# Issuing the sampling weights' four loads of a half band one a slot, right behind the preceding product of weights

## The chip, the core and the metric

The kernel runs on one core of one Trainium2 chip. The metric is the device time of one launch in microseconds; before the change it is 9640.8 us (median of three runs, 9635.6 to 9673.78). All arithmetic is fp32. The engines are named as in the profile: PE (matrix products), PEld (its weight loads), DVE (elementwise work on vectors), ACT (activations and copies), POOL (elementwise work and its own transfers) and SP, which only issues transfers (DMAs).

## The reference

Two layers work on 32 images of 96 channels, 56x56. Layer 0 is an inverted-residual block: a 1x1 convolution to 576 channels, batch norm and SiLU, a depthwise 3x3 convolution, batch norm and SiLU, a squeeze-and-excite gate, a 1x1 convolution back to 96 channels, and the residual. Layer 1 computes magnitudes of a 2-D real FFT of its input, from them and from channel sums a channel gate and a spatial gate, the gated image y, then a 3x3 convolution of y and four coordinate planes that yields 18 offsets and a gate, a plain 3x3 convolution of y, and a deformable one:

```python
y = x * ca * sa
offset = _conv(aux, off_w, off_b, (1, 1))
y_base = _conv(y, base_w, base_b, (1, 1))
px = xx + off[:, :, 0]; py = yy + off[:, :, 1]
sampled = _grid_sample_taps(y, px, py)          # bilinear, 9 taps a pixel
y_def = jnp.einsum('bcthw,oct->bohw', sampled, def_w.reshape(c, c, 9))
z = (1 - gate) * y_base + gate * y_def
```

z is then normalised over the whole batch, x is added, and a ReLU follows.

## The kernel before

**What is computed for the weights.** An image is worked in 7 bands of 8 rows (`bands`, 224 in all), and each band in two halves of 28 columns (h = 0, 1; 448 halves). The bilinear sampling is done by PE: for a 4x4 tile of pixels and one tap each, the values come from an 8x8 block of y around the tile, and the sample is a product of that block (`yt`, 64 positions by 96 channels, transposed from a copy `ybl` of y) with a table of weights over the 64 positions. The weight of a position is a row factor times a column factor. `offsets` makes the factors: PE convolves (`joint_conv`, L605 and L633), DVE copies the offsets out of PSUM (`at`, L651), POOL writes them to DRAM (`od`, L655), SP reads them back spread over partitions (`ht`, L667), ACT turns them into hat functions in two passes (L670, L671), and ACT writes these to DRAM (`hd`, L674). `weights_load` then reads each half's factors back, widened over the 64 positions: `wc` (column factors) and `wr` (row factors), each in two transfers, four of 252 KB for a half, all issued by SP (L685, L686). `weights` multiplies them on DVE (L692, 128x1008, in place in `wc`), and `sample_tiles` uses the product as the moving operand of 14 matrix products (L721; the profile has two rows for each fp32 product), 6 of them in the half's first part, 8 behind its third slot.

**Order.** The main loop runs over the 224 bands and the two halves. A half has 7 slots, a band 17 (7, 7, and 3 behind the halves). In each slot one step of `offsets` for the band after next is issued (`next(more)`), and `pump` issues what is due of two other streams that work on other images: `second(b + 1)` (the rest of layer 0 and the FFTs: transfers `hq` L305, `x2` L361) and `first(b + 2)` (layer 0's depthwise convolution, with DVE's long row L261, transfers `xt` L212 and, from ACT, `h2d` L223). `refill` (transfers `yp` L584 and L596) comes behind the last slot of a band. SP's queue is in exactly this written order (`manual_schedule`), and a transfer that has to wait holds up all that stand behind it. On the other engines a scheduler orders the instructions from their dependences and its own estimate of when their inputs are there; so the place of a product on DVE follows from where its loads are written.

**Buffers.** `wc` has three (READY + AHEAD + 1), `wr` two (AHEAD + 1). Call L the running number of a half, and (j, h) its band in the image and its half. The loads of half L can be issued when `hd` of its band has landed, the tile products of half L-3 have been read out of the `wc` buffer (L721), and the product of half L-2 has been read out of the `wr` buffer (L692). At the top of half L-1 `prepare` issues all four loads of half L; behind the third slot of half L-1 its product is issued. The steps of `offsets` for band n + 2 run during band n: its `od` is issued in the first slots, its `ht` in the first slot of the second half, and its `hd` behind the fourteenth slot.

The transfers of SP and of ACT share eight completion semaphores in turn; an issue waits for the one that used its semaphore eight transfers before.

Of the kernel before, what the change touches and what calls it, by code (L numbers as in the profile page):

```python
# [64 lines left out]
AHEAD = 1  # L65
READY = 1
# [50 lines left out]
def bank(p):  # L117
    return p["mm"].tile([128, 512], FP, name="mm")
# [559 lines left out]
def weights_load(nc, p, hd, h):  # L678

    src = hd.rearrange("n i t k -> n i (t k)")[:, :, h * NTH * KP : (h + 1) * NTH * KP]  # L680
    wc = p["wc"].tile([2 * NS, NTH * KP], FP, name="wc")
    wr = p["wr"].tile([2 * NS, NTH * KP], FP, name="wr")
    for s in range(2):
        ps = slice(s * NS, (s + 1) * NS)
        nc.sync.dma_start(wc[ps], src[2 * s].unsqueeze(0).to_broadcast([SB, SB, NTH * KP]))  # L685
        nc.sync.dma_start(wr[ps], src[2 * s + 1].unsqueeze(1).to_broadcast([SB, SB, NTH * KP]))  # L686
    return wc, wr


def weights(nc, wc, wr):  # L690

    nc.vector.tensor_tensor(wc, wc, wr, ALU.mult)  # L692
    return wc


def block_channels(nc, p, yp, j, h):

    yt = p["yt"].tile([2 * NS, NTH, C], FP, name="yt")
    yb = p["ybl"].tile([C, NTH, 2, SB, SB], FP, name="ybl")
    src = yp[:C, j * RB : j * RB + SB, h * NTH * TS : h * NTH * TS + SB]  # L700
    for s in range(2):
        blocks = bass.AP(src.tensor, src.offset + s * TS * WY, [src.ap[0], [TS, NTH], [WY, SB], [1, SB]])
        nc.gpsimd.tensor_copy(yb[:, :, s], blocks)  # L703
    for lo, hi in ((0, 4), (4, NTH)):
        pt = bank(p)
        for t in range(lo, hi):
            nc.tensor.transpose(pt[:, (t - lo) * C : (t - lo + 1) * C], yb[:, t].rearrange("c s r x -> c (s r x)"),  # L707
                                p["w"]["ident"][:C, :C])
        nc.scalar.copy(yt[:, lo:hi].rearrange("p t c -> p (t c)"), pt[:, : (hi - lo) * C])  # L709
    return yt  # L710


def sample_tiles(nc, p, yt, s, v, group):


    pts = [(bank(p), bank(p)) for _ in group]
    for (lo, hi), pt in zip(group, pts):
        for t in range(lo, hi):
            for k in range(2):
                ps = slice(k * NS, (k + 1) * NS)  # L720
                nc.tensor.matmul(pt[k][:C, (t - lo) * KP : (t - lo + 1) * KP], yt[ps, t], s[ps, t * KP : (t + 1) * KP],  # L721
                                 start=True, stop=True)
    for (lo, hi), pt in zip(group, pts):
        for k in range(2):
            nc.scalar.copy(v[:C, :, lo:hi, k].rearrange("c k t p -> c t k p"),  # L725
                           pt[k][:C, : (hi - lo) * KP].rearrange("c (t k p) -> c t k p", t=hi - lo, k=NTAP))


def pack(nc, v):

    for i in range(3):
        nc.scalar.copy(v[C:, 1 + 2 * i : 3 + 2 * i], v[i * QC : (i + 1) * QC, KA:])  # L732
# [25 lines left out]
def gates_of(nc, p, hid):  # L758

    pgs = bank(p), bank(p)  # L760
    for i, pg in enumerate(pgs):
        ps = slice(i * NS, i * NS + DMID)
        nc.tensor.matmul(pg[:C, :BW], p["w"]["dg2p"][ps], hid[ps], start=True, stop=True)
    return [gate_from(nc, p, pg) for pg in pgs]
# [174 lines left out]
def layers(tc, a, dp, x1d, zd, stats, far):  # L939
# [6 lines left out]
    nc = tc.nc  # L946
    B = x1d.shape[0]
    with ExitStack() as ctx:
        p = {"tc": tc, "dp": ctx.enter_context(tc.tile_pool(name="l1d", bufs=3, space=DRAM))}
# [28 lines left out]
        def flush():  # L978
            while later:
                later.pop(0)[1]()  # L980
# [27 lines left out]
        def start(b, length):  # L1008
            streams[:] = [[second(b + 1), 0, n_second, slot + 3, slot + length - 8],
                          [first(b + 2), 0, n_first, slot, slot + length]]  # L1010

        def pump():
            nonlocal slot
            slot += 1
            for st in streams:
                due = st[2] * min(1.0, (slot - st[3]) / (st[4] - st[3]))
                while st[1] < due:
                    st[1] += 1
                    next(st[0], None)
            later.sort(key=lambda e: e[0])  # L1020
            while later and later[0][0] <= slot:
                later.pop(0)[1]()

        def drain():
            for st in streams:
                for _ in st[0]:
                    pass
# [3 lines left out]
        def refill(b, upto):  # L1031

            upto = min(H, upto)
            r = filled.get(("y", b), 0)
            while ("sa", b) in p and r < upto:
                r1 = min(upto, r + RB)
                args = load_rows(nc, p, yp, b, x1d[b], r, r1)
                later.append((slot + 4, lambda args=args: attend_rows(nc, p, b, *args)))
                r = filled["y", b] = r1
            r = filled.get(("fq", b), 0)  # L1040
            if ("fq", b) in p and r < upto:
                load_freq(nc, p, yp, b, r, upto)
                filled["fq", b] = upto
# [11 lines left out]
        def end_half(n, h, v, gate, st):  # L1055
            if h == 0:
                pds[n] = p["pd"].tile([128, 512], FP, name="pd")
            deform(nc, p, pds[n], v, h)
            if h:
                pd = pds.pop(n)  # L1060
                later.append((slot + 2, lambda: join(n, pd, gate, st)))
# [12 lines left out]
        hids, gates, ybs, hds, ready = [], [], [], [], []  # L1074

        def find(n):
            if n % 2 == 0:
                hids.append(p["hid"].tile([2 * NS, BW], FP, name="hid"))
            hid = hids[n // 2][n % 2 * NS : n % 2 * NS + DMID]
            return offsets(nc, p, yp, bands[n][1], top[:, n % NBD : n % NBD + 1], hid, ybs, hds)  # L1080
# [6 lines left out]
        flush()  # L1087
        p.pop("diag")
        n_loads = 0
        loads = []  # L1090

        def prepare(upto):

            nonlocal n_loads
            while n_loads < min(upto, 2 * len(hds)):
                n, m = divmod(n_loads, 2)
                loads.append(weights_load(nc, p, hds[n], m))
                n_loads += 1

        prepare(READY + AHEAD)  # L1100
        for _ in range(READY):
            ready.append(weights(nc, *loads.pop(0)))
        yts = [block_channels(nc, p, yp, 0, 0)]
        start(0, turn * (NTX + 2))
        for n, (b, j) in enumerate(bands):
            if j == 0:
                st = p["st"].tile([C, NBD, 6], FP, name="st")
            if j == turn:
                drain()
                refill(b + 1, j * RB - PD)  # L1110
                flush()
                start(b + 1, slots)
            more = find(n + 2) if n + 2 < len(bands) else iter(())
            next(more, None)
            for h in range(2):
                v = p["vp"].tile([128, NTAP, NTH, 2, TP], FP, name="v")
                prepare(2 * n + h + READY + AHEAD)
                s = ready.pop(0)
                yt = yts.pop(0)
                for i, group in enumerate(GROUPS):  # L1120
                    sample_tiles(nc, p, yt, s, v, group)
                    for _ in range(group[0][0], group[-1][1]):
                        next(more, None)
                        pump()
                    if i == 0:
                        for end in ends:
                            end()
                        ends.clear()
                        if h == 1 and n + 1 < len(bands):
                            yts.append(block_channels(nc, p, yp, bands[n + 1][1], 0))  # L1130
                        ready.extend(weights(nc, *ws) for ws in loads[:1])
                        del loads[:1]
                        if h == 0:
                            yts.append(block_channels(nc, p, yp, j, 1))
                pack(nc, v)
                if h == 0:
                    if n % 2 == 0:
                        gates.extend(gates_of(nc, p, hids[n // 2]))
                    gate = gates.pop(0)
                ends.append(lambda n=n, h=h, v=v, gate=gate, st=st: end_half(n, h, v, gate, st))  # L1140
            for _ in more:
                pass
            pump()
            pump()
            pump()
            if b + 1 < B:
                refill(b + 1, (j + 1) * RB - PD if j < NBD - 1 else H)
            if j == NBD - 1:
                nc.vector.tensor_reduce(top[:, NBD:], top, AX.X, ALU.max)
# [350 lines left out]
```

## Time and profile before

| | |
|---|---|
| median of three runs | 9640.8 us (9635.6 to 9673.78) |
| profiled execution | 9648.5 us, span 9646.7 us, mean granted PE clock 0.923 |
| PE busy | 8472.7 us (88%) |
| DVE busy | 7227.2 us (75%) |
| ACT busy | 5322.1 us (55%) |
| POOL busy | 2532.6 us (26%) |
| moved by DMA | 1485.98 MB, 154 GB/s over the span |
| products of weights (L692, DVE) | 448 times, 564.6 us busy, 704.2 us idle just before them |

The time of the profiled execution is that of the span and 1.8 us around it. Shares of busy time are over the whole span; the main loop is the stretch from about 480 us to 9350 us, 282 us an image, with a start of one image's layer 0 ahead of it and the normalisation behind it. PE's spans count its own time for a matrix product; the granted clock says in what part of full speed these ran. A row of the waits gives the engine and line that waited, who ended the wait, the sum in us, how often, and the longest.

### The profile page before, as it was taken

How to read it: one execution, taken by the hardware profiler on the slowest of the kernel's cores; microseconds unless marked ns; L12 is line 12 of the kernel's file. 1: busy time of each engine (PE TensorE's matmuls, PEld its weight loads, DVE VectorE, ACT ScalarE, POOL GpSimd, SP SyncE). 2: the span in 40 equal slices, each digit the busy share in tenths (PEclk: the TensorE clock that was granted, in tenths of full speed). 3: DMA queues.
4: the chain of work that ended last, by engine and by line, in shares of the span. 5: the costliest groups of instructions: out<-in, count | busy, mean ns of one | idle time of the engine just before them, and what ended most of it. 6: DMA issues, size and time to landing. Idle time of an engine off the chain costs nothing. (4 is left out here: it accounts for less than half of the span.)

```text
span 9646.7 us, 129705 instructions
## 1 busy us (share of the span) xinstructions
PE 8472.7 (88%) x48374; PEld 5064.2 (52%) x48374; DVE 7227.2 (75%) x6948; ACT 5322.1 (55%) x10262; POOL 2532.6 (26%) x2642
## 2 busy tenths in 40 slices
PE   6889989998999999999899989999999999999870
PEld 3455555555555555555555555555555555555540
DVE  7688777778777787877777887777878777777323
ACT  2355555565555556555555655555555555565453
POOL 1123223222222322222232322233222323322210
PEclk9899999999999999999999999999999999999985
DMA  2355555555555555555555555555555555554449
GB/s 94 95 143 148 151 152 160 150 149 143 147 155 154 160 154 145 145 149 155 154 160 155 145 142 153 151 158 154 153 139 145 150 157 157 153 152 135 130 154 417
DMA packets 1069473, 1485.98 MB, mean 154 GB/s; under 512 B 590438, under 2 KB 840086, under 8 KB 1056550
## 3 DMA queue, kind: packets, MB, share of 16 engines
q1 hardware_dynamic: 858747, 985.20, 37.9%
q10 hardware_dynamic: 153803, 329.80, 9.2%
q0 software_dynamic: 56288, 162.60, 6.7%
q8 instruction: 388, 6.36, 0.3%
q14 instruction: 247, 2.02, 0.1%
HBM read 1064.29 MB, written 412.65 MB: 153 GB/s over the span
## 5 line engine op out<-in xcount | busy, mean ns | idle before, releaser
L261 DVE SCALAR_TENSOR_TENSOR acch<-hp,w,acch 128x1512 f32<-128x1512 f32 (+1 forms) x2250 | 4320.5, 1920 | 32.8
L605 PE MATMUL mm<-yp,c_jointW 104*128 104x448 f32 x4032 | 1649.0, 561 | 9.0 <-ACT yt L709 5.5
L740 PE MATMUL pd<-v,c_def 128*96 128x224 f32 (+1 forms) x6272 | 1414.8, 376 | 127.6 <-ACT v L732 104.1
L703 POOL COPY ybl<-yp 96x448 f32<-96x448 f32 x896 | 1014.7, 1159 | 1903.7 <-PE mm L707 1903.3
L721 PE MATMUL mm<-wc,yt 64*96 64x144 f32 x12544 | 1168.1, 308 | 153.5 <-DVE yb L638 76.8
L740 PEld LDWEIGHTS pd<-v,c_def 128*96 128x96 f32 (+1 forms) x6272 | 1051.8, 173 | 437.4 <-ACT v L732 142.5
L168 PE MATMUL mm<-xt,w 96*128 96x392 f32 (+3 forms) x2688 | 1136.3, 561 | 133.8 <-ACT yt L709 96.0
L605 PEld LDWEIGHTS mm<-yp,c_jointW 104*128 104x128 f32 x4032 | 783.6, 196 | 806.0 <-issue 762.6
L721 PEld LDWEIGHTS mm<-wc,yt 64*96 64x96 f32 x12544 | 884.2, 167 | 489.8 <-issue 188.0
L221 ACT ACTIVATE acch<-acch,sh,inv 128x1568 f32<-128x1568 f32 x288 | 487.5, 1693 | 1159.0 <-DVE acch L261 1143.9
L692 DVE TENSOR_TENSOR wc<-wc,wr 128x1008 f32<-128x1008 f32 x448 | 564.6, 1260 | 704.2 <-DMA wr<-hd 690.5
L725 ACT COPY v<-mm 96x288 f32<-96x288 f32 (+1 forms) x2688 | 1003.6, 442 | 117.7 <-PE mm L721 78.9
L172 ACT ACTIVATE hp<-mm,sh,inv 128x392 f32<-128x392 f32 (+2 forms) x1216 | 811.8, 672 | 326.9 <-PE mm L168 282.1
L633 PE MATMUL mm<-yp,c_base0W 96*64 96x448 f32 x4032 | 913.5, 550 | 0.0
L323 PE MATMUL mm<-hq,w3s 128*96 128x392 f32 x2048 | 788.2, 531 | 127.4 <-DMA hq<-h2d 125.9
L655 POOL DMA_DIRECT2D od<-at x224 | 186.3, 832 | 2275.1 <-DVE at L651 1451.9
L732 ACT COPY v<-v 32x448 f32<-32x448 f32 x1344 | 755.3, 562 | 30.3
L168 PEld LDWEIGHTS mm<-xt,w 96*128 96x128 f32 (+1 forms) x2688 | 389.9, 189 | 495.1 <-issue 264.8
L709 ACT COPY yt<-mm 128x384 f32<-128x384 f32 (+1 forms) x896 | 350.9, 441 | 491.5 <-PE mm L707 489.4
L323 PEld LDWEIGHTS mm<-hq,w3s 128*96 128x96 f32 x2048 | 336.3, 173 | 477.7 <-issue 382.5
L466 POOL TENSOR_TENSOR o<-o,xc 96x392 f32<-96x392 f32 x256 | 396.5, 1549 | 643.9 <-ACT o L333 642.3
L633 PEld LDWEIGHTS mm<-yp,c_base0W 96*64 96x64 f32 x4032 | 294.6, 134 | 515.5 <-issue 490.2
(194 smaller groups left out, 9023.7 us busy)
## 6 DMA issues: line engine op xcount, KB each, us to landing
h2d<-acch ACTq DMA_DIRECT2D x288, 784.0 KB
wc<-hd SPq DMA_DIRECT2D x896, 252.0 KB
wr<-hd SPq DMA_DIRECT2D x896, 252.0 KB
hq<-h2d SPq DMA_DIRECT2D x128, 980.0 KB
hq<-h2d SPq DMA_DIRECT2D x128, 784.0 KB
x<-x1d SPq DMA_DIRECT2D x768, 98.0 KB
ht<-od SPq DMA_DIRECT2D x224, 252.0 KB
hd<-ht ACTq DMA_DIRECT2D x224, 252.0 KB
```

The lines of the kernel that those rows point to most:

```text
L168: nc.tensor.matmul(pt[p0 : p0 + w1.shape[1], : rows * W], w1, xts[hf][:, r0 * W : (r0 + rows) * W], start=True, stop=True)
L172: nc.scalar.activation(h1[lo:hi, row0 : row0 + rows, 1 : 1 + W], pt[lo:hi, : rows * W].rearrange("p (h w) -> p h w", h=rows), AF.Silu, bia ...
L261: nc.vector.scalar_tensor_tensor(acc[:, lo:hi], win, wk, acc[:, lo:hi], ALU.mult, ALU.add)
L323: nc.tensor.matmul(pts[half][:C, :EW], w3s[:, ch], hq, start=(i == 0), stop=False)
L605: nc.tensor.matmul(view, weights[:, k], yp[:channels, r0 : r0 + RB, dx + PD - 1 : dx + PD - 1 + W], start=(k == 0), stop=(k == NTAP - 1))
L633: nc.tensor.matmul(pb[k % 2 * BC : (k % 2 + 1) * BC, :BW].rearrange("p (h w) -> p h w", h=RB), w["base"][:, k], yp[:C, r0 : r0 + RB, dx + ...
L692: nc.vector.tensor_tensor(wc, wc, wr, ALU.mult)
L703: nc.gpsimd.tensor_copy(yb[:, :, s], blocks)
L721: nc.tensor.matmul(pt[k][:C, (t - lo) * KP : (t - lo + 1) * KP], yt[ps, t], s[ps, t * KP : (t + 1) * KP], start=True, stop=True)
L725: nc.scalar.copy(v[:C, :, lo:hi, k].rearrange("c k t p -> c t k p"), pt[k][:C, : (hi - lo) * KP].rearrange("c (t k p) -> c t k p", t=hi - ...
L732: nc.scalar.copy(v[C:, 1 + 2 * i : 3 + 2 * i], v[i * QC : (i + 1) * QC, KA:])
L740: nc.tensor.matmul(out.rearrange("c q (t x) -> c t q x", x=TS), p["w"]["def"][ks, k], v[ks, k].rearrange("c t s (r x) -> c t (s r) x", r=T ...
```

## The change

`weights_load` becomes a generator: it takes the two tiles first, and then issues one transfer a step. `prepare` puts the generator into a list `spread`; `spread_load` advances it. `prepare` is called behind the product of half K+1 (third slot of half K), for half K+2, where it was called at the top of half K for half K+1. In each later slot one transfer is issued ahead of that slot's other work, so the four transfers of a half stand in slots 3, 4, 5 and 6 of the half two before it. A call ahead of the product issues what should be left. The first two halves' loads are issued at once, as before. Number and size of the transfers, the buffers and the products stay as they are.

```diff
@@ weights_load
+    yield wc, wr
     for s in range(2):
         ps = slice(s * NS, (s + 1) * NS)
         nc.sync.dma_start(wc[ps], src[2 * s].unsqueeze(0).to_broadcast([SB, SB, NTH * KP]))
+        yield
         nc.sync.dma_start(wr[ps], src[2 * s + 1].unsqueeze(1).to_broadcast([SB, SB, NTH * KP]))
-    return wc, wr
+        yield
@@ layers
-        loads = []
+        loads, spread = [], []
+
+        def spread_load(steps):
+            for _ in range(steps):
+                while spread and next(spread[0], spread) is spread:
+                    spread.pop(0)
 
         def prepare(upto):
 
             nonlocal n_loads
             while n_loads < min(upto, 2 * len(hds)):
                 n, m = divmod(n_loads, 2)
-                loads.append(weights_load(nc, p, hds[n], m))
+                spread.append(weights_load(nc, p, hds[n], m))
+                loads.append(next(spread[-1]))
                 n_loads += 1
 
         prepare(READY + AHEAD)
+        spread_load(8 * (READY + AHEAD))
@@ the main loop
                 v = p["vp"].tile([128, NTAP, NTH, 2, TP], FP, name="v")
-                prepare(2 * n + h + READY + AHEAD)
                 s = ready.pop(0)
                 yt = yts.pop(0)
                 for i, group in enumerate(GROUPS):
                     sample_tiles(nc, p, yt, s, v, group)
                     for _ in range(group[0][0], group[-1][1]):
+                        spread_load(1)
                         next(more, None)
                         pump()
@@ behind the third slot of a half
+                        spread_load(4)
                         ready.extend(weights(nc, *ws) for ws in loads[:1])
                         del loads[:1]
+                        prepare(2 * n + h + 1 + READY + AHEAD)
```

## The prediction

> **What bounds the kernel now.** I read the page's busy times, then the waits of the engines and of SP's queue, and then one image in the timeline. "Place (j, h)" below is the product for half h of band j of an image.
>
> ```profile
> PE 8472.7 (88%) x48374; PEld 5064.2 (52%) x48374; DVE 7227.2 (75%) x6948; ACT 5322.1 (55%) x10262; POOL 2532.6 (26%) x2642
> ...
> L692 DVE TENSOR_TENSOR wc<-wc,wr 128x1008 f32<-128x1008 f32 x448 | 564.6, 1260 | 704.2 <-DMA wr<-hd 690.5
> ```
>
> ```profile
> DVE wc L692 <- DMA wr<-hd: 690.5, 152, 18.3
> ...
> PE mm L323 <- DMA hq<-h2d: 125.9, 31, 9.4
> ...
> PE mm L707 <- ACT sq L413: 80.3, 21, 6.5
> ```
>
> PE is the limit: between 480 and 9350 us it is busy 8124 of 8870 us. The product's 690 us are DVE's; they count only where they starve PE. They are not spread evenly. Summed by place over the images, 182 us lie at (2,1), 182 at (6,0), 102 at (1,0), 97 at (0,0), and 132 at the ten others. PE's idle time in the loop, 739 us, lies elsewhere: I followed each gap over 0.3 us back through its releasers, and 171 us at (2,1) end at a late `wr`, 125 us at (0,0) at a late `hq`, 47 us at (1,0) at a late `ht`; 312 us end at no transfer. At (6,0), where DVE waits longest, PE idles 0.0 us. One image (the seventeenth), at (2,1), in the timelines of SP, DVE, ACT and PE:
>
> ```profile
> 5060.03 0.57 SPq L686 DMA_DIRECT2D wr<-hd  x1
> 5074.72 0.66 SPq L667 DMA_DIRECT2D ht<-od  x1
> 5075.48 0.57 SPq L685 DMA_DIRECT2D wc<-hd  x1
> ...
> 5077.59 0.57 SPq L686 DMA_DIRECT2D wr<-hd  x1
> ```
>
> ```profile
> 5079.67 1.04 DVE L259 TENSOR_SCALAR acch<-hp,w 128x1568 f32<-128x1568 f32 x1
> 5089.44 1.21 DVE L692 TENSOR_TENSOR wc<-wc,wr 128x1008 f32<-128x1008 f32 x1 [8.73 <-DMA wr<-hd]
> ```
>
> ```profile
> 5091.29 1.00 ACT L413 ACTIVATE sq<-mm 128x464 f32<-128x464 f32 x2 [9.64 <-DVE s L414]
> ```
>
> ```profile
> 5091.90 0.74 PE L707 MATMUL mm<-c_ident,ybl 96*128 96x96 f32 x3 [6.19 <-ACT sq L413]
> ```
>
> SP stands at `ht` until `od` has landed (issued 5067.61, landed 5074.70, behind eight weight loads issued from 5055.6 to 5060.6); the loads of (2,1) follow it and land at 5089.31. DVE, which executes in order, stops at the product 8.73 us; ACT waits for DVE, PE for ACT. Of DVE's stop 2.5 us are hidden from PE. And PE is slow afterwards (columns: busy us of PE, PEld, DVE, ACT, POOL; granted clock; DMA share; GB/s):
>
> ```profile
> 5060.00:5083.00 23.00, 23.00 (x205) 13.62 (x204) 19.96 (x21) 14.31 (x28) 4.83 (x4) 1.00 0.53 136
> ...
> 5089.00:5106.00 17.00, 11.68 (x33) 6.34 (x34) 15.34 (x12) 13.02 (x24) 2.67 (x2) 0.51 0.09 26
> ```
>
> The granted clock is 1.00 before the gap and 0.51 for 17 us behind it. In the records of the loop it is either 1.0 or 0.5, and an L605 product follows the last after 0.383 us at 1.0, after 0.750 us at 0.5. So half of PE's busy time at half clock is lost: 271 us busy so at (2,1) cost 135 us, 114 at (0,0) 57 us, 48 at (1,0) 24 us.
>
> **The change, part by part.** It issues the same 1792 loads (0.57 to 0.60 us each on SP, which has time) and runs the same 448 products. What moves is their place.
>
> On SP, in the order in which the changed program stands: the loads of (1,0) come ahead of six `x2` loads and those of (1,1) ahead of six or four more; (0,0)'s first load ahead of an `hq`; (0,1)'s ahead of an `hq` (the first of them) and three refills; (3,1)'s ahead of six `x2` and three refills; (4,0)'s ahead of two or four `x2`; (6,0)'s and (6,1)'s among the two `hq`; (3,0)'s and (5,0)'s ahead of `xt`. Those of (2,0) and (2,1) pass nothing. On DVE the products move forward: by 14.7 us at (1,0), 12.4 at (2,0), 10.3 at (5,1), 10.1 at (6,0), 5 to 6 at (0,1), (1,1), (4,0), 2 to 5 at (0,0), (4,1), (6,1) (medians: time between the end of the row that will precede it and its present arrival), and not at (2,1), (3,0), (3,1), (5,0). A product that moves forward gains only if its loads move as far.
>
> *Place (2,1).* Its neighbours stay. But ahead of it (1,1)'s loads come some 7 to 19 us sooner, so the burst of eight is gone: `od`, whose usual landing takes 3.2 us (the page's median), no longer takes 7.1, and `ht` is free 3.9 us sooner, less 1.2 us since (1,1)'s product now stands ahead of `at`. The buffer of `wc` is the next limit: the tile products of (1,0) end at 5072.87, so the loads go at 5072.9 and not 5075.5. 2.6 us sooner at least, 4.3 if the transfers ahead are done too; 3.5 x 31 images = 108 us of PE's idle 171 (bounds 0 and 171). The clock's part in the same proportion: 85 of 135 us.
>
> *Place (0,0).* The `hq` that PE waits 3.81 us for landed 13.2 us after its issue, behind another `hq` (980 KB), four weight loads and an `ht`. Two of the four, 504 KB, now go ahead of the waiting first `hq`. At the 3024 KB that went from 4988.8 to 5007.25 (164 KB/us) that is 3.1 us; I take 2.7 x 31 = 85 us (bounds 62, at the window's 256 GB/s, and 125), and 35 us of clock.
>
> *Place (1,0).* ACT waits for an `ht` that was issued behind four loads and took 10.5 us; a lone one took 3.8 us (issued 5116.57). 35 of 47 us, and 12 us of clock; bounds 0 and 71.
>
> *New costs.* At (6,0) the loads now wait for `hd` itself: it was issued by ACT at 5213.32 and landed at 5224.73, behind (5,1)'s loads. These now go at 5200.5 (when the tile products of (4,0) release their buffer), so I let `hd` land at 5217; with the `hq` among them the four loads are in by about 5229 to 5230. DVE reaches the product at 5225.3: a stop of 4.5 us in place of 5.5, but now ahead of `at`, `yb` and the gate's scaling, where DVE idles 2.40 and 3.65 us anyway. `at` is late by 5 us, and ACT's copies queue behind it; PE has no idle time there to show its margin. Between 0 and 31 x 5 = 155 us I take 45. At (2,0) the product comes 8.9 us ahead of the old landing; its loads go 2.5 us sooner and without the burst, 4 to 8 us more: a stop of 0 to 2 us, 15 us. The last `x2` of the second FFT have 3.9 to 5.2 us between landing and use, and two weight loads of 1.9 us each now ahead: 15 us (0 to 60). `hq` (5 to 14 us of margin elsewhere), refills (3.6 us and more, and their use on DVE moves behind the product) and `xt` hide. ACT gets two table loads more, 2 x 1.28 us.
>
> *Sum.* -(108 + 85 + 85 + 35 + 35 + 12) + 45 + 15 + 15 + 3 = -282 us. Not all of it reaches the end: from (6,0) to (0,1) ACT waits up to 10 us for DVE's depthwise rows, and 312 us of PE's idle time hang on such chains. I take a third back (bounds: none, and all of (0,0)'s 120 with half the rest), which leaves -188 us. 9648.5 - 188 = 9460 for the profiled execution; that one stands 7.7 us above the median of the runs, so 9453.
>
> The Trainium skill (TensorE: Matmul & The Clock Gate, Part 1) has the clock at half after an idle window of about 3.4 us and back after a busy one of the same length. This trace's 17 us at half clock behind a 6.19 us gap are longer than that, as PE kept starving. By the page a gap left at 6.19 - 3.5 = 2.7 us would cost no clock at all, and the 135 us of (2,1) would all come back, 50 us more than in my sum. The same skill (DMA: Bandwidth & Descriptors, Queues, rings and completion order) says that a transfer's semaphore rises only after all earlier writes of that DMA engine, across its queues; that speaks against the change, since loads moved ahead of small transfers delay these, and with `hd` and `od` as late as now the gain at (2,1) would be the buffer's 2.6 us or less.
>
> **The rivals.**
>
> *Slower: the products outrun their loads.* Place (6,0): if `hd` still lands at 5224.7, the loads land 3.3 us sooner than now, but the product comes 15.6 us ahead of the old landing; DVE stops 12 us in place of 5.5, 6.4 us more, and at (2,0), where it stops nowhere now, up to 6.4. 12.8 x 31 = 400 us of DVE; at (2,1) PE lost 171 of 182 such us and 135 of clock, so with half of that hidden under PE's backlog, +340 us, less 220 of the 360 us of gains kept: about 9760. It decides once `hd` of (6,0) lands later than some 5221. For it: scheduler estimates, not landings, placed the products. Against: what delayed `hd` are loads that leave.
>
> *No change.* `od` and the buffer keep (2,1) as it is, and at (0,0) PE's head start is lost to DVE: only (1,0) and a part of (0,0) stay, -50 us less the new costs: 9630. For it: nothing moves at (2,1). Against: the burst ahead of it does.
>
> *Much faster.* All idle time of the three places and its clock go, (171 + 125 + 47) + (135 + 57 + 24) = 559 us, with the 78 us of costs and a third back -321: about 9320.
>
> **How the numbers follow.** Likeliest 0.62 (its own range 9330 to 9570), much faster 0.06, no change 0.14, slower 0.18. What a measurement can tell from no change is about 0.5%, 48 us. Faster 0.68, same 0.14, slower 0.18. The range runs from 9310 to 9700: it leaves out a few in a hundred below and most of the slower case.
>
> **What would show it.** Right: DVE's wait for `wr` falls from 690 us to 250 to 400, with (1,0) and (0,0) near zero; PE's wait for `hq` falls below 50 us; the gap of L707 behind L413 below 3 us; the granted clock of the loop rises from 0.94 to 0.95 or more. Wrong: DVE waits at (6,0) or (2,0) for longer than now, with `hd` late; or PE's waits for ACT and DVE (L740, L721, L168) grow by what `hq` loses.

## The result and the profile after

The changed kernel takes 9817.8 us (median of four runs, 9805.7 to 9831.5) against 9650.3 us of before (four runs in the same comparison): 1.0164 times the time, 95% interval 1.0139 to 1.0188. The forecast was 9453 us, 2% faster. The profiled execution took 9805.65 us with a span of 9803.6 us, 157 us more than the one of before, at a mean granted clock of 0.909 in place of 0.923.

Page of the changed kernel (L692 has become L694, L721 L723, L740 L742):

```profile
PE 8618.4 (88%) x48374; PEld 5134.8 (52%) x48374; DVE 7279.0 (74%) x6948; ACT 5324.3 (54%) x10264; POOL 2593.3 (26%) x2642
...
L694 DVE TENSOR_TENSOR wc<-wc,wr 128x1008 f32<-128x1008 f32 x448 | 551.7, 1231 | 600.4 <-DMA wr<-hd 571.6
```

Waits of the engines, changed kernel:

```profile
DVE wc L694 <- DMA wr<-hd: 571.6, 126, 22.7
...
ACT yb L628 <- DVE at L651: 304.5, 121, 8.7
...
PE mm L723 <- DVE yb L638: 142.1, 85, 4.0
...
PE mm L323 <- DMA hq<-h2d: 95.3, 31, 8.1
```

The two middle ones in the kernel before:

```profile
ACT yb L628 <- DVE at L651: 128.0, 70, 5.2
...
PE mm L721 <- DVE yb L638: 76.8, 55, 6.1
```

The change does a part of what it should: DVE waits 119 us less for the loads, PE 31 us less for `hq`. But PE waits 65 us more for DVE's `yb` and ACT 177 us more for DVE's `at`. And the busy time of PE has risen by 146 us with the same matrix products. That is nearly the whole 157 us, and it is the clock. Main loop of before, then of after (columns as in the prediction: busy us of PE, PEld, DVE, ACT, POOL; granted clock):

```profile
480.00:9350.00 8870.00, 8124.46 (x46983) 4868.60 (x46983) 6808.87 (x6343) 5080.91 (x9907) 2475.76 (x2564) 0.94 0.54 149
```

```profile
480.00:9508.00 9028.00, 8270.97 (x46989) 4941.47 (x46987) 6861.43 (x6343) 5083.48 (x9913) 2537.01 (x2565) 0.92 0.55 147
```

PE's idle time in these two windows is nearly the same, 746 us and 757 us (the window less PE's busy time). I laid 29 images of each trace over each other, from one image's product of place (0,0) to the next one's. The time PE spent at half clock rose from 34.8 to 44.1 us an image, half of which, 4.7 us, is lost; its idle time from 23.1 to 23.3; the image from 282.9 to 287.4 us. The added half clock lies mainly at 220 to 250 us (0.1 us before, 7.2 us after; PE's idle time there went from 0.0 to 1.8 us). That is behind place (6,0), where PE was never idle before. Place (6,0) of one image in the changed kernel, timelines of DVE and of PE:

```profile
5318.91 0.69 DVE L651 COPY at<-mm 18x224 f32<-18x224 f32 x2 [1.69 <-ACT hid L625]
5319.63 0.61 DVE L662 TENSOR_REDUCE top<-at 18x1 f32<-18x448 f32 x1
5326.49 1.21 DVE L694 TENSOR_TENSOR wc<-wc,wr 128x1008 f32<-128x1008 f32 x1 [6.25 <-DMA wr<-hd]
5327.62 0.61 DVE L638 TENSOR_TENSOR yb<-yb,mm 64x448 f32<-64x448 f32 x1
```

```profile
5325.14 0.73 PE L723 MATMUL mm<-wc,yt 64*96 64x144 f32 x8
5328.28 1.28 PE L723 MATMUL mm<-wc,yt 64*96 64x144 f32 x8 [2.41 <-DVE yb L638]
```

The same place in the kernel before, DVE:

```profile
5229.06 0.62 DVE L638 TENSOR_TENSOR yb<-yb,mm 64x448 f32<-64x448 f32 x1 [2.40 <-ACT yb L636]
5233.33 0.17 DVE L292 TENSOR_TENSOR s<-acc,seb 128x5 f32<-128x5 f32 x1 [3.65 <-PE acc L290]
5233.77 0.17 DVE L294 TENSOR_SCALAR s<-s 128x5 f32<-128x5 f32 x1 [0.27 <-ACT s L293]
5233.98 0.66 DVE L296 TENSOR_TENSOR w3s<-w,s 128x480 f32<-128x480 f32 x1
5240.10 1.21 DVE L692 TENSOR_TENSOR wc<-wc,wr 128x1008 f32<-128x1008 f32 x1 [5.46 <-DMA wr<-hd]
```

DVE stops for about as long in both, 6.25 and 5.46 us. Before, it stopped behind `yb`, and only DVE's own depthwise rows stood behind it. Now it stops ahead of `yb` in all 29 images, and in 15 of them ahead of `at` too. `yb` reads the base convolution's PSUM bank, and PE waits for `yb`: 2.41 us idle, and in this image the clock went to half at 5327.5, inside this gap, for 10.2 us.

### The profile page after: what moved, and what is told of

It is laid out like the page before. It is cut to its first block, busy times and chain, and to the rows that moved or that the text cites. A ratio compares the mean times of both kernels' runs of the same rounds, so it can differ in the third digit from the quotient of the medians.

```text
span 9803.6 us, 129787 instructions
## 1 busy us (share of the span) xinstructions
PE 8618.4 (88%) x48374; PEld 5134.8 (52%) x48374; DVE 7279.0 (74%) x6948; ACT 5324.3 (54%) x10264; POOL 2593.3 (26%) x2642
## 5 line engine op out<-in xcount | busy, mean ns | idle before, releaser
L605 PE MATMUL mm<-yp,c_jointW 104*128 104x448 f32 x4032 | 1662.3, 565 | 11.0 <-DMA yp<-fqd 9.8
L705 POOL COPY ybl<-yp 96x448 f32<-96x448 f32 x896 | 1079.9, 1232 | 2047.5 <-PE mm L709 2047.1
L742 PE MATMUL pd<-v,c_def 128*96 128x224 f32 (+1 forms) x6272 | 1503.6, 391 | 101.8 <-ACT v L734 68.4
L723 PE MATMUL mm<-wc,yt 64*96 64x144 f32 x12544 | 1214.0, 316 | 226.0 <-DVE yb L638 142.1
L742 PEld LDWEIGHTS pd<-v,c_def 128*96 128x96 f32 (+1 forms) x6272 | 1095.2, 181 | 468.3 <-ACT v L734 117.0
L723 PEld LDWEIGHTS mm<-wc,yt 64*96 64x96 f32 x12544 | 914.4, 172 | 586.7 <-issue 215.0
L605 PEld LDWEIGHTS mm<-yp,c_jointW 104*128 104x128 f32 x4032 | 788.6, 197 | 816.3 <-issue 756.2
L694 DVE TENSOR_TENSOR wc<-wc,wr 128x1008 f32<-128x1008 f32 x448 | 551.7, 1231 | 600.4 <-DMA wr<-hd 571.6
L323 PE MATMUL mm<-hq,w3s 128*96 128x392 f32 x2048 | 768.0, 520 | 99.4 <-DMA hq<-h2d 95.3
L259 DVE TENSOR_SCALAR acch<-hp,w 128x1568 f32<-128x1568 f32 x270 | 314.2, 1164 | 479.8 <-ACT hp L172 477.8
```

Source lines behind the costliest of these rows:

```text
L323: nc.tensor.matmul(pts[half][:C, :EW], w3s[:, ch], hq, start=(i == 0), stop=False)
L605: nc.tensor.matmul(view, weights[:, k], yp[:channels, r0 : r0 + RB, dx + PD - 1 : dx + PD - 1 + W], start=(k == 0), stop=(k == NTAP - 1))
L742: nc.tensor.matmul(out.rearrange("c q (t x) -> c t q x", x=TS), p["w"]["def"][ks, k], v[ks, k].rearrange("c t s (r x) -> c t (s r) x", r=T ...
```

## The experiments

"Place (j, h)" is, as in the prediction, the product for half h of band j. A point is one per cent of the time of the kernel before. `early(...)` in the diffs lets only the named places' loads go early; the others are issued at once at the top of the half before use, as in the kernel before. Ratios are to runs of the kernel before on the same chip (medians 9671.6 to 9678.8 us there; only ratios are compared between groups).

**Place (6,0) held**

```diff
+        def early(load):
+            place = load // 2 % NBD, load % 2
+            return place != (6, 0)
...
+                prepare(2 * n + h + READY + AHEAD)
+                spread_load(8)
                 s = ready.pop(0)
...
-                        prepare(2 * n + h + 1 + READY + AHEAD)
+                        if early(2 * n + h + READY + AHEAD):
+                            prepare(2 * n + h + 1 + READY + AHEAD)
```

> As the changed kernel, but the four loads of place (6,0) are issued at once at their old place (top of half (5,1)); on DVE its product goes back to 1 row ahead of its old place instead of 5.5. Theory A (place (6,0): DVE stops ahead of `yb`, PE waits for `yb`, its clock halves): between 220 and 250 us of each image the half clock goes from 7.2 us back to about 0, PE's wait of L721 for `yb` from 142 us to about 80, and the time from 9818 to about 9680 (+-30). Theory B (the slowdown is spread over all moved places, (6,0) is a third of the added 280 us at half clock): about 9765.

Measured: 9717.4 us, ratio 1.0047 (1.0032 to 1.0062). Half clock at 220 to 250 us of an image: 2.2 us; PE's wait for `yb` 128.8 us. 1.2 of the 1.6 points are gone with this place's loads alone, less than theory A's 1.4 and more than theory B's 0.5. Theory A's half clock of about 0 and wait of about 80 us were not reached: the product is back at its old place in 14 of the 29 images, and in 14 it stands two rows ahead of that, inside the gate's scaling.

**Place (6,0) alone**, on the kernel before: the same edit with `return place == (6, 0)`.

> As the kernel before, but the loads of place (6,0) alone are issued early, one a slot; on DVE its product moves 3 rows forward, nothing else moves on DVE. Theory A: slower than before by 100 to 140 us, about 9770, with half clock at 220 to 250 us of each image. Theory B: slower by some 50 us, about 9700.

Measured: 9778.3 us, ratio 1.0103 (1.0075 to 1.0131), 101 us slower. One place out of fourteen, with the loads' number and size unchanged, costs two thirds of what the whole change costs. All of it lies behind this place: at 220 to 250 us of an image PE is idle 2.7 us (0.0 before) and at half clock 3.1 us (0.1 before). But theory A's wait for `yb` is not what PE lost it by. The product moved by only three rows: it stays behind `yb` and stops DVE ahead of `s`, the first row of the gate's scaling (L292), for 7.3 us on average where the stop in the old place was 5.9. ACT waits for `s` (this run, then before), and its copies of `v` stand behind that in its own queue:

```profile
ACT s L293 <- DVE s L292: 160.3, 32, 8.4
```

```profile
ACT s L293 <- DVE s L292: 14.6, 32, 2.6
```

PE waits for these copies for 189.5 us (L742), 104.1 us before; its wait for `yb` is 67.8 us, 76.8 before. The rule is the same, the row behind the stop is another.

**All early loads at once**

```diff
                         prepare(2 * n + h + 1 + READY + AHEAD)
+                        spread_load(8)
```

> As the changed kernel, but the four loads are issued at once right behind the preceding product, not one a slot: early without spread. Products move a little further forward on DVE (7 rows at (6,0), 14.5 at (5,0)). Theory A: (6,0) stays, so 9800 to 9850. If the spreading itself cost (loads between others on SP's queue), this is faster than 9818 by more than 50 us. If `hq` and `x2` behind four loads cost, slower by 50 us or more.

Measured: 9850.4 us, ratio 1.0179 (1.0147 to 1.0210), at the upper end of theory A's forecast and not told apart from the changed kernel (1.0139 to 1.0188). Issuing one a slot is not what costs.

**Product of (6,0) late, loads early**

```diff
-                        ready.extend(weights(nc, *ws) for ws in loads[:1])
-                        del loads[:1]
+                        if (j, h) != (5, 1):
+                            ready.extend(weights(nc, *ws) for ws in loads[:1])
+                            del loads[:1]
...
+                if (j, h) == (5, 1):
+                    ready.append(weights(nc, *loads.pop(0), tc))
                 pack(nc, v)
```

With `tc`, `weights` keeps its product behind the DVE rows written before it (`tc.keep_in_program_order`).

> As the changed kernel, with its order of SP's transfers, but the product of place (6,0) is issued at the end of half (5,1) and kept behind the DVE rows written before it, so that it stands behind `yb` and the gate's scaling again (two rows behind its place before the change). If what costs at (6,0) is the product's place on DVE, this is as fast as the run that holds the loads, about 9680. If it is SP's queue (`hq` and `ht` behind loads that wait for `hd`), it stays near 9818.

Measured: 9652.9 us, ratio 0.9978 (0.9963 to 0.9993). All transfers of SP and all rows of POOL and PE stand in the changed kernel's order, and so do all of DVE's rows but this product, six rows later, and the one of (6,1), about one row; on ACT 30 of 10844 stand elsewhere. The product of one place stands behind `yb` again, and 1.9 points of the time are back (1.0164 to 0.9978, some 180 us). What cost was the product's place on DVE, not SP's queue. Half clock at 220 to 250 us is 0.7 us. At its new place the product no longer stops DVE (0.2 us an image).

So the rest of the change was worth 0.2%. The next runs ask where the other gains went.

**Product of (2,1) in written order**, on the kernel before, all loads as before: `weights(nc, *ws, tc if (j, h) == (2, 0) else None)`.

> The kernel before, with one thing changed: the product of place (2,1) is kept behind the DVE rows written before it, which puts it 22 rows later on DVE; all loads stay. Theory (the stop at (2,1) costs PE 5.5 us of idle time an image and half a clock behind it): DVE's wait for `wr` falls by about 180 us, PE's idle time at 80 to 100 us of an image from 5.9 to about 1 us, the half clock at 80 to 110 us from 11.4 to 3 us, together 4.9 + 4.2 = 9 us an image, 280 us; a third may come back as other waits, so 9400 to 9480. Rival (PE has nothing else to do there, the idle time only changes its releaser): within 50 us of before.

Measured: 9415.6 us, ratio 0.9735 (0.9717 to 0.9753). The image is 8.3 us shorter; PE's idle time fell by 4.2 us an image and its half clock by 9.1. All of that lies at (2,1): PE's idle time at 80 to 100 us of an image fell from 5.8 to 1.4 us, its half clock at 80 to 110 us from 11.4 to 2.0 us. The loop's granted clock is 0.95:

```profile
480.00:9110.00 8630.00, 8009.53 (x46990) 4811.23 (x46988) 6827.42 (x6343) 5088.12 (x9909) 2640.87 (x2565) 0.95 0.56 153
```

The reading of (2,1) was right, and its price near (256 us measured, 280 expected). What mends it is to put the product where its loads are there, without touching a load. The scheduler also moved some later rows, of DVE 579 of 6500, most of them by one place, so the run has a new order behind that product, and not that product alone elsewhere.

**Both of these, with early loads everywhere** (the two edits above on the changed kernel).

> Early loads one a slot, product of (6,0) late (9653 in its own run) and product of (2,1) kept in written order. If the two are independent: as much faster than 9653 as the run with (2,1) alone is faster than before.

Measured: 9396.0 us, ratio 0.9714 (0.9693 to 0.9735): 2.6 points below the run with the late product of (6,0), as expected of independent places.

**(4,0) held**, with the late product of (6,0): `return place != (4, 0)`.

> Early loads one a slot, product of (6,0) late, and the loads of (4,0) at their old place, behind the six `x2`. If `x2` behind two or four loads is what eats the rest of the gain: POOL's gating gets `x2` in time, PE's wait of L386 for POOL falls from 83 to about 35 us, half clock at 150 to 170 us of an image from 5.3 to 2.5 us, and 9653 falls by 40 to 90 us. Else within 20 us of 9653.

Measured: 9584.1 us, ratio 0.9901 (0.9876 to 0.9926), 0.8 points below the run without the hold. PE's wait for POOL's gated `x2` is 32.5 us (82.8 without the hold, 34.3 before). Early loads at (4,0) cost some 75 us. That they do it by delaying `x2` fits the 50 us of PE's wait, but is not shown alone: the product of (4,0) moved back by three rows too (its stop, 12 to 14 us in sum, hardly changed).

**The candidate**: early loads only at `(0, 0), (0, 1), (1, 0), (1, 1), (6, 0)`, the product of (6,0) late, that of (2,1) in written order.

> The candidate: early loads only at (0,0), (0,1), (1,0), (1,1) and (6,0) (product late there), the others at their old place, and the product of (2,1) in written order. It should have the gains of the run with (2,1) alone and lose nothing at (4,0) to (5,1): the fastest of the four, some 30 to 90 us below the run with (2,1) alone.

Measured: 9293.6 us, ratio 0.9601 (0.9575 to 0.9627), 122 us below the run with (2,1) alone, more than expected. In the loop the granted clock is 0.96:

```profile
480.00:8990.00 8510.00, 7945.48 (x46989) 4754.83 (x46989) 6861.82 (x6343) 5086.03 (x9904) 2665.60 (x2565) 0.96 0.57 156
```

**The first four places alone**, on the kernel before: `return place in ((0, 0), (0, 1), (1, 0), (1, 1))`.

> The kernel before, with early loads one a slot at (0,0), (0,1), (1,0) and (1,1) alone; no product is held. This is the part of the change that the prediction credited at (0,0) and (1,0). Theory (these places gain, (4,0) to (6,1) lose): faster than before by 60 to 120 us, with the half clock at 0 to 60 us of an image from 12 to 9 us and PE's idle time there from 8.4 to 6 us. Rival (early loads gain nothing anywhere without (2,1) mended): within 30 us of before.

Measured: 9550.5 us, ratio 0.9864 (0.9836 to 0.9892), 128 us faster. Half clock at 0 to 60 us fell from 12.1 to 8.5 us, PE's idle time there from 8.5 to 6.2. These places do gain by early loads.

**The candidate, at once**: `spread_load(8)` behind its `prepare`.

> The candidate (9294), with the four loads of its early places issued at once and not one a slot. If the spreading matters there, slower by 30 us or more; if only the early place matters, the same; at (0,0) all four loads then stand ahead of the `hq` that PE waits for, where one a slot puts one of them, which is worth up to 90 us (PE's wait for `hq`, 93 us).

Measured: 9323.8 us, ratio 0.9633 (0.9608 to 0.9659), not told apart from the candidate's.

**The candidate, (0,0) at once**

```diff
                             prepare(2 * n + h + 1 + READY + AHEAD)
+                            if (j, h) == (6, 0):
+                                spread_load(8)
```

> The candidate, with the loads of (0,0) alone at once. If three loads ahead of `hq` are what is left of PE's wait for it: that wait falls from 93 to under 30 us, half clock at 0 to 10 us from 2.2 to about 0.5, and the time by 60 to 110 us, to about 9210. If the wait only changes its releaser: within 25 us of 9294.

Measured: 9314.4 us, ratio 0.9615 (0.9584 to 0.9646). Waits of PE, this run and then the candidate:

```profile
PE mm L725 <- DVE yb L638: 194.4, 64, 8.0
...
PE mm L323 <- DMA hq<-h2d: 8.4, 4, 6.2
```

```profile
PE mm L725 <- DVE yb L638: 98.3, 52, 11.8
...
PE mm L323 <- DMA hq<-h2d: 93.0, 30, 7.3
```

The wait for `hq` is gone, and all of it is back as a wait for `yb`. In the overlaid images PE's idle 2.9 us at 0 to 10 us became 0.0, and the 1.9 us at 30 to 50 us became 5.2, with 5.7 us more of half clock at 30 to 60 us. Taking the wait away moved it some 35 us on, to the next thing that was late. In the 15 us before these later waits DVE is idle only 0.8 us on average: mostly it is behind with its rows, not stopped.

**The candidate without (6,0)**: early loads at the first four places, product of (2,1) in written order.

> The candidate without its change at (6,0): early loads at the first four places, product of (2,1) in written order, (6,0) as before. If the stop at (6,0) costs PE nothing in its old place (PE idle 0.0 us there), this equals the candidate within 25 us; if the DVE time freed at (6,0) reaches PE, it is slower by up to 60 us.

Measured: 9287.0 us, ratio 0.9588 (0.9562 to 0.9614), as fast as the candidate with one edit less; this is the version to keep. DVE's stop at (6,0) in its old place costs PE nothing that can be measured here.

**Idle time and clock together.** For each run: the length of an image, PE's idle time in it, its time at half clock (us, means of 29 images), and what the sum of idle time and half of the half clock changed against before:

```
run                          image   idle   half clock   image -before   idle + half/2 -before
before                       282.9   23.1   34.8
after                        287.4   23.3   44.1         +4.6            +5.0
(6,0) held                   284.5   23.2   38.6         +1.7            +2.1
(6,0) alone                  286.9   25.8   38.1         +4.1            +4.4
at once                      289.6   25.4   46.5         +6.7            +8.2
(6,0) late                   282.7   21.9   37.1         -0.1            +0.0
(2,1) in written order       274.6   18.8   25.7         -8.3            -8.8
both                         273.9   18.9   23.5         -9.0            -9.8
(6,0) late, (4,0) held       280.3   20.7   34.0         -2.6            -2.8
candidate                    270.2   16.7   21.4         -12.6            -13.0
first four                   279.3   20.5   33.5         -3.5            -3.2
candidate, at once           271.3   17.5   23.2         -11.5            -11.4
candidate, (0,0) at once     271.9   16.9   24.5         -11.0            -11.3
candidate without (6,0)      270.3   16.5   21.3         -12.6            -13.3
```

An image is PE's busy and idle time together in any case, and PE does the same products in every run. What the last two columns show is that its busy time changes with half of the half clock: within 0.8 us an image in every run but the all-at-once one, where they say 1.5 us too much.

## Why the prediction was wrong

*What bounds the kernel* held: PE with its clock, and DVE's 690 us only where they starve PE. The run with (2,1) in written order gave most of the price that was read for that place (171 us of idle time and 135 us of clock; 256 us measured).

*New costs, (6,0)* is the step that failed. Its pieces came out much as forecast: `hd` lands 4.7 us sooner (forecast 7.7), the loads land at 226.7 us of the image where DVE comes to the product at 222.2, the stop is 4.7 us (means of 29 images; forecast 4.5). Its price, "between 0 and 31 x 5 = 155 us I take 45", was not: some 180 us, more than the upper bound, come back when the product alone is put behind `yb` again (1.9 points of ratio). The step granted PE a margin for late `at` and `yb` because PE had no idle time there. No idle time showed only that nothing had been late yet, and a gap's clock, counted at (2,1) and (0,0), was left out at this place.

*Place (2,1)*, 193 us forecast, gave little. On average over the images `ht` went 4.9 us sooner, more than forecast, but the loads of (2,1) only 2.2 us sooner, where 3.5 us were taken. The buffer of `wc` is released by the tile products of (1,0): the 2.6 us between their end and the first load were read from one image, the mean was 1.0 us, and in the changed kernel it is 0.03 us. And DVE, whose arrival was held fixed, also came 2.0 us sooner. The stop is 5.5 us in place of 5.8; PE's idle time at 80 to 100 us of an image fell from 5.8 to 4.4 us, but its half clock at 80 to 110 us rose from 11.4 to 13.1 us. A fourth buffer for `wc` was not tried.

*Place (0,0)*, 120 us forecast: the step counted two of four loads ahead of the waiting `hq`, though its own listing of SP's order says one. One, 252 KB, went; `hq` took 11.7 us from issue to landing in place of 13.0 (medians), PE's wait fell by 31 us. And where all four go ahead, the wait reappears at `yb`, as the third taken back supposed for this place.

*Places (0,0) to (1,1) together* were right in sign and near in size: 128 us alone on the kernel before, against 167 forecast for (0,0) and (1,0). That the size is near is in part luck. In that run idle time and half of the half clock fell by 1.7 us an image at 0 to 10 us, some 53 us where 120 were forecast for (0,0), and by 2.8 us at 30 to 60 us, some 87 us where 47 were forecast for (1,0). The stop at (1,0) went from 102 to 6 us in sum.

*`x2` behind the loads of (4,0)*: 15 us taken, range to 60; 75 us measured, if all of it is `x2`'s.

Of the rivals, the slower one had the right place and the right sign, "the products outrun their loads" at (6,0), but not its condition: `hd` did land early, so by its own deciding point it should not have come. DVE's stop did not grow. It moved ahead of work that PE waits for. Of the waits named as signs of being wrong, only that of L723 for DVE grew clearly (`yb`, 65 us more); that of L742 for ACT's `v` fell from 104.1 to 68.4 us. Put together, from ratios of runs: first four -1.4 points, (6,0) +1.9, (4,0) +0.8, which sums to +1.3 of the +1.6 measured. The three were taken from different kernels ((6,0) alone on the kernel before is +1.0), so the sum is rough; the other eight places' share was not run one by one.

The Trainium skill (TensorE: Matmul & The Clock Gate, Part 1) puts the return to half clock at an idle window of about 3.4 us, and the prediction drew from it that a gap of 2.7 us costs no clock. The traces differ: of the gaps from 2.5 to 3.0 us that began at full clock, 3 of 8 before and 14 of 26 after the change were followed by half clock (see below). The small transfers that the prediction feared for: in four of the seven bands the median of `od` from issue to landing rose from about 3.0 to 5.4 us or more, in one it fell from 6.2 to 2.9 us; that of the `hd` of (6,0) fell from 10.8 to 2.6 us.

## What to carry to other kernels

When loads are moved earlier, look first at what their consumer is now ahead of in its own in-order queue: a scheduler that believes the loads are there moves the consumer with them, and the same stop then holds up other work. A stop on an engine off the critical path is harmless only at its present place; if it cannot be removed, place it behind what the bounding engine waits for (here one product kept in written order was worth 2.6%, with no load moved). Price a gap of PE with the clock that follows it, and read a margin as a median over repetitions, not from one of them.

## What the runs showed of the hardware

Many PE gaps of 1.5 to 2.5 us were followed by half clock. In 29 images of each trace I counted the gaps that began at full clock, and those of them that half clock followed at once (it began during the gap or within 1 us of its end):

| gap | before | after |
|---|---|---|
| 0.2 to 1.0 us | 5 of 166 | 10 of 200 |
| 1.0 to 1.5 us | 15 of 58 | 2 of 81 |
| 1.5 to 2.5 us | 33 of 69 | 45 of 103 |
| 2.5 to 3.0 us | 3 of 8 | 14 of 26 |
| 3.0 to 3.5 us | 21 of 28 | 12 of 12 |
| over 3.5 us | 35 of 36 | 19 of 20 |

What else decides for the shorter gaps, no run here shows. Half clock lasts 3.4, 6.8, 10.2, 13.7 or 17.1 us, steps of 3.4 us (one stretch of the changed kernel lasts 23.9 us), so the gap of 2.41 us at (6,0) was followed by 10.2 us of it. At half clock products follow each other at nearly twice the interval (L605: 0.750 us and 0.383 us). So PE's busy time rose by 146 us in a kernel that does the same products, with 12 us more of idle time.
